# Attention with conditioned queries and keys: the order of small operations at the start and at the end of the kernel

## The chip, the cores and the metric

The kernel runs on one core of a Trainium2 chip. A core has TensorE (PE in the profile; PEld is its weight load), VectorE (DVE), ScalarE (ACT), GpSimd (POOL) and SyncE (SP, which here only issues transfers). Each engine works through its own instructions in the order in which the program issues them, and waits on semaphores for the others. The metric is the device time of one execution in microseconds (us), less is better.

## The reference, cut to what matters

```python
# x: (8, 512, 512), cond: (8, 512); 16 heads of 32
Q, K, V = heads(x @ Wq.T + bq), heads(x @ Wk.T + bk), heads(x @ Wv.T + bv)
tQ, tK  = heads(cond @ Wq.T + bq), heads(cond @ Wk.T + bk)   # one token per batch
scores  = einsum("bhqd,bhkd->bhqk", Q + tQ, K + tK) / sqrt(32)
out     = x + merge(einsum("bhqk,bhkd->bhqd", softmax(scores), V))
```

All in float32. The condition adds one vector per batch and head to every query and to every key; the residual x is added at the end.

## The kernel before

The work is cut into 32 tiles: tile t is batch t // 4 and four heads (t % 4). For each tile the kernel projects queries and keys, computes scores twice (once with queries as rows for the row maxima and the sums of exponentials, once with keys as rows for the exponentials that are multiplied with V), multiplies and stores. The main loop runs over tiles 1 to 28; the opening (tile 0 and the weights) and the last three tiles (29, 30, 31) are written out by hand. A manual schedule keeps each engine's order as written, so the place of a statement in the program is its place in the queue of its engine. The eight PSUM banks are given out by a table (`TURNS`, `banks`); a matmul that writes a bank waits for those who still read it.

Opening. TensorE first runs fillers, small matmuls whose result nobody reads (`keep_warm`, L892; `WARM = (48, 8, 8)`). x of batch 0 arrives in two halves of its rows; VectorE turns each half by two transposes of 128x512 (`turn_first_x`, L903, L908). `project` multiplies with the first columns of Wq and Wk. The second group of 8 fillers stands between the projections of the two halves, the third between the last projection of tile 0's queries and the first scores (`row_max(0, 0)`). `condition` (L863) makes tQ and tK: 32 small matmuls per weight (L870), a VectorE transpose (L878), and per group of heads one addition of `bias2` on ScalarE (L880). `bias2` is made by two VectorE scalings (L928, L929) of the turned condition (L924). W of q, k and v are turned by VectorE (`turn_w`, L342) once they have landed. Sums and differences of their blocks are made by GpSimd (`combine_w`, L361 to L364), for products of blocks in Strassen's manner, seven in place of eight: `first_products` (L496) and `other_products` (L563) issue them (L469) and put them together. In `first_products` ScalarE copies product one out of its bank (L507), then come the exponentials that were passed as `dens` (`denominators`, L682), and then what was passed as `small`. `row_max` issues the scores (L635) and VectorE's maxima (L602, L644). `split_max` (L696 to L699) cuts the maxima into three bf16 parts, which TensorE transposes (L722).

End. `crossed` (L1178 and on) interleaves the two kinds of scores for neighbouring tiles; the maxima are L1213 and L644. `part_of` (L1007) adds up the products with V: the first part of a tile is copied to SBUF by ScalarE (L1022), a later one is copied by ScalarE (L1016) and added by GpSimd (L1017). `send_parts` (L1030) divides by the sums: reciprocal (L1032), VectorE's transpose (L830), GpSimd's product and addition of the residual (L831, L832); `store` issues the transfers (L850). `add_bias` (L209, GpSimd) adds bv to the residual. For tiles 30 and 31 the sums of exponentials come from TensorE products with a matrix of ones (`times_ones`, L773) over sums that VectorE or GpSimd made first (`sum_of`, L1167, L1169). Tile 30's result is `y30`: transposed, scaled (L1294), the residual added (L1326), stored by `store_30` (L1299). Tile 31 ends with L1309 to L1341: the product and the residual added (L1319), TensorE transposes of it (L1321) and of the sums (`untranspose`, L854), the reciprocal (L1329), the scaling (L1334), and four stores (L1341).

Of the kernel before, what the change touches and what calls it, by code (L numbers as in the profile page):

```python
# [17 lines left out]
def kernel(  # L18
# [38 lines left out]
    nc = tc.nc  # L57
# [17 lines left out]
    WARM = (48, 8, 8)  # L75
# [787 lines left out]
    def condition(n, gs, pt):  # L863

        i = "qk".index(n)
        r = slice(gs[0], gs[-1] + 1)
        w = len(gs) * HD
        for cc in range(NC):
            for h in range(HG):
                nc.tensor.matmul(  # L870
                    pt[h * HD : (h + 1) * HD, :w],
                    condT[:, cc, :],
                    wT[n][:, cc, :].rearrange("p (g h e) -> p g h e", h=HG, e=HD)[:, r, h, :],
                    start=(cc == 0),
                    stop=(cc == NC - 1),
                )
        t = early[:, 1 + i, :w]
        nc.vector.transpose(t, pt[:, :w])  # L878
        for k, g in enumerate(gs):
            nc.scalar.activation(  # L880
                tok[:, i, g, :],
                t[:, k * HD : k * HD + B],
                AF.Identity,
                bias=bias2[:, i, g : g + 1],
            )
        if gs[-1] == G - 1:
            nc.gpsimd.tensor_tensor(apart_tok[:, i], tok[:, i, 1::2], tok[:, i, 0::2], ALU.subtract)
# [4 lines left out]
    def keep_warm(n):  # L892
        for _ in range(n):
            nc.tensor.matmul(warm[:, :P], onesb, onesb, start=True, stop=True)
# [8 lines left out]
    def turn_first_x(half):  # L903
        if half == 0:
            xT[0] = xtp.tile([P, NC, S], F32, tag="xT", name="xT_0")
        for k in range(2):
            cs = slice(k * 2, k * 2 + 2)
            nc.vector.transpose(  # L908
                xT[0][:, cs, two[half]].rearrange("p c (f i) -> p c f i", i=BL),
                x0[:, half_of_x[half], cs, :].rearrange("p f c e -> p c f e"),  # L910
            )
# [16 lines left out]
    nc.vector.tensor_scalar(bias2[:, 0, :], condT[:, :, B], 2.0 * SCALE, None, ALU.mult)  # L928
    nc.vector.tensor_scalar(bias2[:, 1, :], condT[:, :, B + 1], 2.0, None, ALU.mult)  # L929
# [11 lines left out]
    keep_warm(WARM[2])  # L941
# [35 lines left out]
    condition("q", [2, 3], banks(2))  # L977
    first_products("q", 0, 1, lambda: denominators(0, 1), lambda: condition("k", [2, 3], banks(3)), 1)
# [28 lines left out]
    def part_of(t, pt, of, between=None):  # L1007
# [5 lines left out]
        if t in parts:  # L1013
# [161 lines left out]
    def row(i):  # L1175
        turn[0] = 8 + i
# [43 lines left out]
    load_residual(t + 1)  # L1220
    row(4)
# [16 lines left out]
    add_bias(t - 1)  # L1238
# [7 lines left out]
    load_residual(t + 1)  # L1246
    for u in (t - 1, t, t + 1):
        add_bias(u)
    part_of(t - 1, banks(2), [2, 3])
    spread_sums(apart, banks(1))  # L1250
    den = denominators_of(t - 1, banks(1))
    row(1)
# [4 lines left out]
    send_parts(t - 1, den)  # L1257
    store()
# [26 lines left out]
    sum_of(t, acc2, 2, nc.vector)  # L1285
# [8 lines left out]
    nc.vector.tensor_tensor(y30, y30, rec.broadcast_to([P, NB, BL]), ALU.mult)  # L1294

# [8 lines left out]
    times_ones(acc2, pd, True, False)  # L1304
    times_ones([es[t, 3, pr] for pr in range(NP)], pd, False, True)
    times_v(t, 3, pv)
# [10 lines left out]
    two = [slice(0, HS), slice(HS, S)]  # L1317
    for i in range(2):
# [5 lines left out]
        if i == 0:  # L1324
            untranspose(den, pi)
    nc.vector.tensor_tensor(y30, y30, x30, ALU.add)  # L1326
    store_30(nc.sync, (0, 1))
    store_30(nc.scalar, (2,))
    nc.vector.reciprocal(  # L1329
        rec, pi.rearrange("p (c h e) -> p c h e", c=NS, h=HG)[:, :, :, 0:1]  # L1330
    )
# [13 lines left out]
    store_30(nc.scalar, (3,))  # L1345

# [30 lines left out]
```

## Time and profile before

| | |
|---|---|
| time, median of 3 runs | 664.89 us (664.83 to 665.09) |
| time of the profiled execution | 664.89 us |
| its span, first to last instruction | 663.1 us |
| mean granted TensorE clock | 0.997 |
| busy: PE / DVE / ACT / POOL | 652.7 / 578.4 / 543.2 / 338.0 us |

A row of the timeline gives start and length in us from the start of the span, the engine, the line of the kernel, the operation, the tiles written and read, and the shape; in brackets stand the idle time of the engine before it and what ended that. Instructions of one line that follow one another are merged (x8). A row of the chain of waits gives start, length, engine, tile and line: the work that, followed back from the last instruction, decided when it ended. Matmuls are pipelined and overlap, so their rows can overlap too. A q behind an engine's name is its queue: a transfer issued there.

### The profile page before, as it was taken

The numbers are of one execution on the slowest core, as the hardware profiler recorded it, in microseconds if no ns is written. First come the engines' busy times: TensorE is split into PE (matmuls) and PEld (weight loads), VectorE is DVE, ScalarE is ACT, GpSimd is POOL, SyncE is SP. The second block draws the span as 40 slices with busy tenths as digits, with TensorE's granted clock in tenths as the row PEclk, the third lists the DMA queues.
The fourth block names the chain that finished last, engine by engine and source line by source line (L and its number), as shares of the span: only waits on it lengthen the run. The fifth ranks groups of instructions, "written<-read, shape, count | busy, mean of one in ns | idle before, by whom it ended". The sixth has DMA issues, their size and how long they took to land.

```text
span 663.1 us, 22865 instructions
## 1 busy us (share of the span) xinstructions
PE 652.7 (98%) x9100; PEld 307.0 (46%) x9100; DVE 578.4 (87%) x845; ACT 543.2 (82%) x1391; POOL 338.0 (51%) x447
## 2 busy tenths in 40 slices
PE   8999999999999999999999999999999999999996
PEld 7454444544445444444544445444544545445431
DVE  5898988989798898979889898998979888897787
ACT  2479797888979888898989889798997978888673
POOL 5642543647537464565635664464744656352360
PEclk9999999999999999999999999999999999999998
DMA  9718548285665838657493865839476573830212
GB/s 210 147 33 211 119 109 211 66 219 118 158 168 123 208 73 222 132 138 184 106 223 74 205 151 129 197 75 233 95 180 154 131 185 67 214 89 16 44 33 33
DMA packets 140815, 90.86 MB, mean 137 GB/s; under 512 B 117436, under 2 KB 126308, under 8 KB 140708
## 3 DMA queue, kind: packets, MB, share of 16 engines
q1 hardware_dynamic: 132196, 73.78, 48.3%
q0 software_dynamic: 5568, 14.95, 8.8%
q8 instruction: 72, 1.18, 0.8%
q10 hardware_dynamic: 2944, 0.66, 0.5%
q14 instruction: 35, 0.29, 0.1%
HBM read 20.27 MB, written 8.39 MB: 43 GB/s over the span
## 4 chain that ended last, share of the span: by engine, by line
PE 94%; DVE 3%; issue 1%; DMA 1%; ACT 1%; ACTq 0%; DVEq 0%
PE psum L469 44%; PE psum L635 19%; PE psum L763 16%; PE psum L741 8%; PE psum L738 3%; PE psum L410 2%; DVE acc L1169 1%; DMA early<-in_x_dram 1%; DVE nmax L644 1%; PE psum L1195 1%; DVE nmax L1213 0%; DVE acc L1167 0%; PE psum L800 0%; PE psum L870 0%; ACT arena L682 0%
## 5 line engine op out<-in xcount | busy, mean ns | idle before, releaser
L602 DVE TENSOR_REDUCE nmax<-psum 128x1 f32<-128x512 f32 x326 | 205.1, 681 | 42.9 <-PE psum L635 42.4
L682 ACT ACTIVATE psum<-psum,nmax 128x512 f32<-128x512 f32 x256 | 169.3, 665 | 46.6 <-DVE nmax L602 34.5
L752 ACT ACTIVATE arena<-psum 128x512 f32<-128x512 f32 x264 | 136.3, 602 | 31.2 <-PE psum L741 22.2
L682 ACT ACTIVATE arena<-psum,nmax 128x512 f32<-128x512 f32 x224 | 152.9, 709 | 4.9 <-issue 4.2
L635 PE MATMUL psum<-kT,qT 32*128 32x512 f32 x1024 | 151.5, 619 | 0.0
L655 DVE STREAM_TRANSPOSE blocks<-blocks 128x1024 f32<-128x1024 f32 x112 | 132.3, 1220 | 0.3 <-DMA blocks<-arena 0.3
L644 DVE TENSOR_REDUCE nmax<-psum 128x2 f32<-128x1024 f32 x87 | 105.5, 1213 | 1.1 <-PE psum L635 1.1
L666 POOL DMA_DIRECT2D blocks<-arena x112 | 55.9, 504 | 72.8 <-ACT arena L682 63.6
L831 POOL TENSOR_TENSOR res<-res,recs 128x512 f32<-128x512 f32 x30 | 31.4, 1047 | 118.8 <-DVE res L830 118.8
L635 PEld LDWEIGHTS psum<-kT,qT 32*128 32x128 f32 x1024 | 55.1, 182 | 62.3 <-issue 17.4
L763 PE MATMUL psum<-arena,v 128*32 128x512 f32 x576 | 69.4, 597 | 0.0
L741 PE MATMUL psum<-qT,kT 32*128 32x512 f32 x528 | 67.9, 587 | 0.0
L682 ACT ACTIVATION_READ_ACCUMULATOR psum<-psum,nmax 128x1 f32 x256 | 52.6, 205 | 0.0
L763 PE MATMUL psum<-blocks,v 128*32 128x256 f32 x896 | 52.1, 381 | 0.0
L682 ACT ACTIVATION_READ_ACCUMULATOR arena<-psum,nmax 128x1 f32 x224 | 50.8, 227 | 0.0
L832 POOL TENSOR_TENSOR xr<-res,xr 128x512 f32<-128x512 f32 x30 | 38.4, 1279 | 2.4
L209 POOL TENSOR_TENSOR xr<-xr,wT_q 128x512 f32<-128x512 f32 x30 | 38.5, 1284 | 0.3
L763 PEld LDWEIGHTS psum<-blocks,v 128*32 128x32 f32 x896 | 26.4, 110 | 25.0 <-ACT arena L752 10.6
L830 DVE STREAM_TRANSPOSE res<-psum 128x512 f32<-128x512 f32 x28 | 20.1, 717 | 19.8 <-issue 16.0
L469 PE MATMUL psum<-wT_v,xT 128*32 128x256 f32 x512 | 34.2, 382 | 0.0
L469 PE MATMUL psum<-wc_v,xc 128*32 128x256 f32 x512 | 33.5, 379 | 0.0
L544 POOL TENSOR_TENSOR v<-v 128x512 f32<-128x512 f32 x14 | 17.9, 1277 | 29.3 <-ACT v L532 29.3
(190 smaller groups left out, 986.4 us busy)
## 6 DMA issues: line engine op xcount, KB each, us to landing
blocks<-arena SPq DMA_DIRECT2D x336, 128.0 KB, 4.1
blocks<-arena POOLq DMA_DIRECT2D x112, 128.0 KB, 4.0
xr<-in_x_dram SPq DMA_DIRECT2D x60, 128.0 KB, 2.7
x<-in_x_dram SPq DMA_DIRECT2D x56, 128.0 KB, 3.5
out_dram<-xr SPq DMA_DIRECT2D x56, 128.0 KB, 2.5
w_q<-in_L_cond_Wq_dram SPq DMA_DIRECT2D x4, 256.0 KB
w_k<-in_L_cond_Wk_dram SPq DMA_DIRECT2D x4, 256.0 KB, 7.3
w_v<-in_L_cond_Wv_dram SPq DMA_DIRECT2D x4, 256.0 KB
```

Of the source, the lines that this page charges most:

```text
L209: nc.gpsimd.tensor_tensor(xr[t], xr[t], bias, ALU.add)
L469: nc.tensor.matmul(pt[r], still[:, r], moving, start=(kc == kcs[0]), stop=(kc == kcs[-1]))
L602: nc.vector.tensor_reduce(nmax[t][:, qc, j : j + 1, 0], pt, AX.X, ALU.max, negate=True)
L635: nc.tensor.matmul(pt, qkT["q", t][r, qc * P : (qc + 1) * P], qkT["k", t][r, :], start=True, stop=True,)
L644: nc.vector.tensor_reduce(nmax[t][:, qc, pr * 2 : pr * 2 + 2, 0], pt, AX.X, ALU.max, negate=True)
L655: nc.vector.transpose(e, e)
L666: queue.dma_start(to.rearrange("p c h s -> p (c h s)"), of)
L682: nc.scalar.activation(to, of, AF.Exp, bias=nmax[t][:, qc, j, :], accum_out=sums[t][:, qc, j, :],)
L741: nc.tensor.matmul(bank[j], qkT["k", t][r, kc * P : (kc + 1) * P], qkT["q", t][r, :], start=False, stop=True,)
L752: nc.scalar.activation(e[:, i, :], bank[pr * 2 + i], AF.Exp)
L763: nc.tensor.matmul(pt[j * HD : (j + 1) * HD, at], vs[b % 2][:, kc, (g * HG + j) * HD : (g * HG + j + 1) * HD], e, start=(kc == chunks[0]), ...
L832: nc.gpsimd.tensor_tensor(xr[t], y, xr[t], ALU.add)
```

## The change

In the opening: the second group of fillers has 4 matmuls instead of 8 and the third is dropped; x's second half is turned by three transposes (two of 128x256, one of 128x512); `bias2` is made by ScalarE; and for heads 2 and 3 the additions of the condition stand behind exponentials in ScalarE's queue, those for q between the second and the third exponential of row 1, those for k behind all of `first_products`.

At the end: the residual of tile 31 is named, and bv added to the residuals of tiles 28, 29 and 31, at the start of tile 29; the last two products of tile 29 are added by one VectorE operation directly from PSUM; tile 29 is sent and stored before the next scores instead of after them; one sum of exponentials of tile 31 (chunk 2) is no longer made by VectorE, TensorE multiplies the exponentials with the ones themselves; `y30` gets its residual right after its scaling and is stored by SP in one go; tile 31's sums are transposed, and their reciprocal taken, before the second half of its result.

```diff
-    WARM = (48, 8, 8)
+    WARM = (48, 4)
...
-    def condition(n, gs, pt):
+    def condition(n, gs, pt, later=False):
...
+        def add():
+            for k, g in enumerate(gs):
+                nc.scalar.activation(tok[:, i, g, :], t[:, k * HD : k * HD + B], AF.Identity, bias=bias2[:, i, g : g + 1])
+            if gs[-1] == G - 1:
+                nc.gpsimd.tensor_tensor(apart_tok[:, i], tok[:, i, 1::2], tok[:, i, 0::2], ALU.subtract)
+        if later:
+            return add
+        add()
...
-        for k in range(2):
-            cs = slice(k * 2, k * 2 + 2)
+        for cs in ((slice(0, 1), slice(1, 2)) if half else (slice(0, 2),)) + (slice(2, 4),):
...
-    nc.vector.tensor_scalar(bias2[:, 0, :], condT[:, :, B], 2.0 * SCALE, None, ALU.mult)
-    nc.vector.tensor_scalar(bias2[:, 1, :], condT[:, :, B + 1], 2.0, None, ALU.mult)
+    for i, scale in enumerate((2.0 * SCALE, 2.0)):
+        nc.scalar.activation(bias2[:, i, :], condT[:, :, B + i], AF.Copy, scale=scale)
...
-    keep_warm(WARM[2])
...
-    condition("q", [2, 3], banks(2))
-    first_products("q", 0, 1, lambda: denominators(0, 1), lambda: condition("k", [2, 3], banks(3)), 1)
+    add_q = condition("q", [2, 3], banks(2), later=True)
+    add_k = []
+    def early_dens():
+        denominators(0, 1, js=range(2))
+        add_q()
+        denominators(0, 1, js=range(2, HG))
+    first_products("q", 0, 1, early_dens, lambda: add_k.append(condition("k", [2, 3], banks(3), later=True)), 1)
+    add_k[0]()
...
-        if t in parts:
+        if directly:
+            nc.vector.tensor_tensor(parts[t], pt, parts[t], ALU.add)
+        elif t in parts:
...
     t = T - 3
     load_residual(t + 1)
+    load_residual(t + 2)
+    for u in (t - 1, t, t + 2):
+        add_bias(u)
...
-    add_bias(t - 1)
+    add_bias(t + 1)
...
-    load_residual(t + 1)
-    for u in (t - 1, t, t + 1):
-        add_bias(u)
-    part_of(t - 1, banks(2), [2, 3])
+    part_of(t - 1, banks(2), [2, 3], directly=True)
     spread_sums(apart, banks(1))
     den = denominators_of(t - 1, banks(1))
+    send_parts(t - 1, den)
+    store()
     row(1)
...
-    send_parts(t - 1, den)
-    store()
     row(2)
...
-    sum_of(t, acc2, 2, nc.vector)
...
+    nc.vector.tensor_tensor(y30, y30, x30, ALU.add)
...
     times_ones(acc2, pd, True, False)
+    times_ones([es[t, 2, pr] for pr in range(NP)], pd, False, False)
     times_ones([es[t, 3, pr] for pr in range(NP)], pd, False, True)
+    store_30(nc.sync, range(HG))
     times_v(t, 3, pv)
...
+    untranspose(den, pi)
...
-            untranspose(den, pi)
-    nc.vector.tensor_tensor(y30, y30, x30, ALU.add)
-    store_30(nc.sync, (0, 1))
-    store_30(nc.scalar, (2,))
-    nc.vector.reciprocal(
-        rec, pi.rearrange("p (c h e) -> p c h e", c=NS, h=HG)[:, :, :, 0:1]
-    )
+            nc.vector.reciprocal(
+                rec, pi.rearrange("p (c h e) -> p c h e", c=NS, h=HG)[:, :, :, 0:1]
+            )
...
-    store_30(nc.scalar, (3,))
```

25 lines of the change are left out of this document (15 added, 10 removed).

## The prediction

> **What bounds the kernel now.** I read the page first (busy shares, chain), then the chain of waits in order of time for the first 45 us and the last 75 us, then the timeline of each engine there, because the diff touches only those two stretches.
>
> ```profile
> span 663.1 us, 22865 instructions
> PE 652.7 (98%) x9100; PEld 307.0 (46%) x9100; DVE 578.4 (87%) x845; ACT 543.2 (82%) x1391; POOL 338.0 (51%) x447
> PE 94%; DVE 3%; issue 1%; DMA 1%; ACT 1%; ACTq 0%; DVEq 0%
> ```
>
> TensorE carries 94% of the chain that ended last. So what it issues earlier in the opening moves the whole middle by the same amount; nothing in the middle is edited. In the opening the chain shows where TensorE spends time on fillers and where it leaves its own work:
>
> ```profile
> 10.80 0.45 PE psum L894 x8
> 11.25 1.94 PE psum L410 x8
> ...
> 15.80 0.45 PE psum L894 x8
> 16.25 1.07 PE psum L635 x8
> ...
> 27.74 1.13 DVE nmax L644
> ...
> 29.06 0.49 ACT tok L880 x2
> 29.55 0.27 ACT qT L507
> ...
> 29.95 1.07 PE psum L469 x16
> ...
> 32.34 3.16 PE psum L469 x56
> ```
>
> Columns: start, length, engine, tile, line. The two L894 pieces are fillers on the chain. Around 29 us the chain leaves TensorE: the condition additions (L880) wait for VectorE's row maxima (L644), and the copy of the first product (L507), queued behind them on ScalarE, holds the next product at 29.95.
>
> At the end the chain passes to VectorE at 633.8 us. These rows are of the timeline (start, length, engine, line, operation; in brackets the idle time before it and what ended it):
>
> ```profile
> 633.80 1.29 DVE L1213 TENSOR_REDUCE nmax<-psum 128x1 f32<-128x512 f32 x2 [1.62 <-PE psum L635]
> 636.30 0.65 DVE L830 STREAM_TRANSPOSE res<-parts 128x512 f32<-128x512 f32 x1
> 636.93 1.29 DVE L1213 TENSOR_REDUCE nmax<-psum 128x1 f32<-128x512 f32 x2
> 639.39 1.22 DVE L696 CAST split<-nmax 128x16 bf16<-128x16 f32 x1
> 640.86 0.20 DVE L698 CAST split<-rest 128x16 bf16<-128x16 f32 x1
> 635.84 2.36 POOL L1167 TENSOR_TENSOR acc<-arena 128x1024 f32<-128x1024 f32 x1
> 638.15 1.05 POOL L831 TENSOR_TENSOR res<-res,recs 128x512 f32<-128x512 f32 x1
> 639.28 1.26 POOL L832 TENSOR_TENSOR xr<-res,xr 128x512 f32<-128x512 f32 x1
> 641.38 0.40 PE L722 MATMUL psum<-identb,split 128*128 128x128 bf16 x4 [1.22 <-DVE split L699]
> ```
>
> See the two casts of the same size: 0.20 us at L698, but 1.22 at L696, which runs from 639.39 to 640.61 while GpSimd's addition L832 runs from 639.28 to 640.54. TensorE stands idle 1.22 us for the split that follows.
>
> **The change part by part: opening.** The rows it needs beside the chain:
>
> ```profile
> 10.43 1.30 DVE L908 STREAM_TRANSPOSE xT<-early 128x512 f32<-128x512 f32 x2 [1.67 <-DMA early<-in_x_dram]
> 11.66 0.27 DVE L924 STREAM_TRANSPOSE early<-early 128x128 f32<-128x128 f32 x1
> 13.90 0.59 ACT L880 ACTIVATE tok<-early,bias 128x8 f32<-128x8 f32 x2 [9.22 <-DVE early L878]
> 14.53 0.69 ACT L425 ACTIVATE kT<-psum,tok 128x512 f32<-128x512 f32 x1
> 29.00 0.61 PE L469 MATMUL psum<-xT,wT_q 128*32 128x256 f32 x8
> L254 SPq DMA_DIRECT2D w_k<-in_L_cond_Wk_dram x4: 902/1038/1148, 9.2 to 12.3; - x4
> w_k<-in_L_cond_Wk_dram SPq DMA_DIRECT2D x4, 256.0 KB, 7.3
> 19.71 0.71 DVE L342 STREAM_TRANSPOSE wT_k<-w_k 128x512 f32<-128x512 f32 x1
> 21.45 0.75 DVE L423 TENSOR_SCALAR qT<-psum,tok 128x512 f32<-128x512 f32 x1 [0.34 <-PE psum L410]
> 22.95 1.28 POOL L361 TENSOR_TENSOR wc_q<-wT_q 128x512 f32<-128x512 f32 x1 [6.06 <-ACT psum L682]
> 39.08 0.26 POOL L696 CAST split<-nmax 128x16 bf16<-128x16 f32 x1 [0.42 <-DVE nmax L644]
> ```
>
> Smaller pieces and four fillers fewer. The projection now waits for the first L908 piece, 10.43 + 0.65 = 11.08. A 128x256 piece lies between 0.27 (128x128) and 0.65 (128x512): 0.40 on a line, so it is there at 10.83. Eight fillers are 0.45, so four end at 10.80 + 0.23 = 11.03: the projection starts 0.22 earlier. One instruction more makes the half 2 x 0.40 + 0.65 = 1.45 instead of 1.30, so the condition's transpose (L924) ends at 12.1; its reader on TensorE, after 11.03 + 1.94 = 12.97, covers that.
>
> The two bias scalings go to ScalarE, which had stood idle 9.22 us. At a third of a us each at most (half of L880's 0.59 is the nearest row) they end by 12.7, ahead of L880 at 13.9: nothing. Without that cover they would cost their 0.6.
>
> The second filler group: 0.45. Its successor, the scores at 16.25, needs kT, ready at 14.53 + 0.69 = 15.22, less the 0.22: no wait appears. TensorE is now 0.67 ahead.
>
> Condition additions behind the exponentials. From 29.00 to 32.34 TensorE does 24 matmuls of L469 and 8 of L635. By the rows at 32.34 (3.16 / 56) and 16.25 that is 24 x 0.056 + 1.07 = 2.42; it takes 3.34, so 0.92 is waiting, first for L507, then for the banks that the late exponentials free. Now the copy runs when the first product is out, before the second one's matmuls at 29.00, and two exponentials run before the additions. The additions' readers come later on VectorE. So up to 0.92; offered in all 1.59, and at least nothing.
>
> What is late next: GpSimd. Its twelve weight combinations run without a gap from 22.95 to the split at 39.08, and had 0.42 to spare there; the split's transposes stood some 0.3 more before their turn (estimate: the split's four operations end near 40.3, TensorE's work before them at 32.34 + 3.16 + 1.07 + 3.16 + 1.07 = 40.80, two rounds of the L469 and L635 rows, less the handover). The combinations begin behind VectorE's turn of wT_q, which stands behind turning w_k at 19.71. The last w_k piece is issued at 12.3 and lands 7.3 later, 19.6, whatever the engines do. So VectorE gains about 0.06 there and 0.34 by not waiting at 21.45: GpSimd starts 0.40 earlier. The opening is worth 0.40 + 0.42 + 0.3 = 1.1 us; ends 0.7 (GpSimd no earlier) and 1.59 (never late).
>
> **End.**
>
> ```profile
> 630.74 1.92 PE L763 MATMUL psum<-arena,v 128*32 128x512 f32 x16
> 650.89 2.35 DVE L1169 TENSOR_TENSOR acc<-acc,arena 128x1024 f32<-128x1024 f32 x2
> 651.37 1.07 PE L763 MATMUL psum<-arena,v 128*32 128x512 f32 x8
> 656.16 0.76 DVE L1319 TENSOR_TENSOR late<-psum,late 128x256 f32<-128x256 f32 x2
> 656.83 0.68 DVE L1326 TENSOR_TENSOR late<-late 128x512 f32<-128x512 f32 x1
> 658.49 1.48 SPq L1341 DMA_DIRECT2D out_dram<-late  x2
> 659.74 0.65 ACTq L1299 DMA_DIRECT2D out_dram<-late  x1
> ```
>
> The part added directly (ScalarE's copy and a GpSimd addition go) costs VectorE about 0.68, as L1326, inside the 1.62 idle before 633.80: from the product's end, 632.66, to 633.4. Then `send_parts` (about 0.2 for the reciprocal and L830's 0.65) to 634.2, which delays the maxima at 633.80 by 0.4. They take 2.4 (from 633.80 to just before L830 at 636.30), so VectorE is free at 636.6. The next maxima, at 636.93, I take to wait for their scores, as the row at 633.80 does: nothing gained, and the 0.4 hidden by the 0.85 that left the place in front of them. Without that cover it would cost the 0.4.
>
> GpSimd: `add_bias` of three tiles moves to the start of tile 29, some 20 us ahead of need (uncovered it would cost three times about L832's 1.26), and the addition goes. So L831, L832 and L1167 run 634.2 + 1.05 + 1.26 + 2.36 = 638.9, done 0.5 before the cast at 639.39. The cast falls to 0.20: 1.02 at L722, within TensorE's 1.22. The bounds are 0 and 1.2. `store()` moves with it on SP, in front of nothing that is due there.
>
> The Trainium skill, "SBUF — State Buffer", section "Who interferes with whom", has a cast able to take the port pair shared with GpSimd, the second to issue being blocked for the whole instruction. By it a GpSimd operation still running at 639.39 takes all of the 1.02 back; with the trace's overlap of L696 and L832 it agrees.
>
> The last sum, 2.35 on VectorE, becomes eight matmuls. TensorE's groups are 1.92 - 1.07 = 0.85 apart, so from the product at 651.37 - 1.02 = 650.35 there are five groups: 4 x 0.85 + 1.07 = 4.47, ended 654.82, and L1319 follows near 654.9 instead of 656.16. Of the 2.35 only 1.25 - 1.02 = 0.23 arrives: TensorE is the bound now. The addition of x to y30 (0.68) and tile 30's stores go into the freed time on VectorE and SP. The reciprocal now stands before the second half's addition and waits for the sums' transposes, in the place that L1326 had; I take L1334 1.2 earlier (from 1.0 to 1.3). Last to be issued was the store at 659.74, behind two others on ScalarE's queue; now it is SP's second L1341, 658.49 + 0.74 - 1.2 - 0.1 (two stores no longer in front of it) = 657.9. So the end gives 1.85, the stores landing alike; ends 0.8 and 2.1.
>
> **Sum.** 664.89 is the profiled execution's own time and the median (span 663.1 and 1.79 around it). 664.89 - 1.1 - 1.85 = 661.94, so 661.9.
>
> **The rivals.** (B) GpSimd's chain still meets the cast: it needs only 0.5 us of delay. For it, the chain starts behind VectorE's transpose; against it, its operations have no other wait. The end gives 1.85 - 1.02 = 0.83: 664.89 - 1.1 - 0.83 = 663.0. (C) The opening is eaten by weights that land at fixed times: turning w_k at 19.71 starts within 0.1 of the landing worked out. GpSimd then starts no earlier and the opening gives 0.7, or nothing where a bank comes free late as well: 664.89 - 1.85 less 0.7 or 0, so 662.3 to 663.0. Against it, the banks' readers move earlier with the copy. B together with an opening that gives nothing: 664.89 - 0.83 = 664.1, within 0.2% (1.33 us, what a measurement can tell from no change). (D) Slower: the clock. If fewer fillers let TensorE fall to half clock in the stretch where they go, 10.80 to 16.25, its 5.45 us of work would take as long again: 664.89 - 2.95 + 5.45 = 667.4; it decides from 3 us of work at half clock. Against it, a row of the view by stretches (length, five engines' busy time with counts, then the granted clock):
>
> ```profile
> 5.50:6.80 1.30, 0.00 (x0) 0.00 (x0) 0.72 (x2) 0.00 (x0) 0.00 (x0) 1.00 0.51 152
> ```
>
> The clock is 1.00 in a stretch where TensorE does nothing for 1.3 us, and the change opens no gap as long. The Trainium skill, "TensorE: Matmul & The Clock Gate", section "What's actually happening", halves the clock after an idle window of about 3.4 us; no gap here reaches that, so by it too the fillers dropped cost nothing.
>
> **How the numbers follow.** Forecast 0.56, B 0.13, C 0.12, B with C 0.10, D and whatever like it I do not see 0.09. Faster 0.81, same 0.10, slower 0.09. Range: the best ends give 664.89 - 1.59 - 2.1 = 661.2, and 0.4 lower for what is priced low; the top is B with C, 664.1: 660.8 to 664.1. The forecast's own range is 661.2 to 662.9.
>
> **What would show it.** Right: first scores near 15.6; product seven without a gap after 29 us less 0.7; the split cast at 0.2 us with GpSimd idle; no VectorE sum after 650; the last issue near 656.8 in the new clock of the span. Wrong: a TensorE gap before the first L722 over 0.6; a cast over 1 us; L1319 less than 0.9 earlier against L722; a granted clock below 1.00 before 30 us.

## The result and the profile after

The changed kernel takes 661.48 us (median of 5 executions, 660.83 to 662.42) where the kernel before takes 664.83 in the same comparison: a ratio of 0.9948, 95% interval 0.9937 to 0.9959. The forecast was 661.9 with a range of 660.8 to 664.1. The profiled execution took 661.48 too, so the 3.41 us to the 664.89 of the profile before can be followed row by row.

The first line of the page of the kernel after, and its shares of the chain that ended last:

```profile
span 659.7 us, 22856 instructions
PE 92%; POOL 2%; DMA 2%; SPq 1%; DVE 1%; issue 1%; ACT 0%; ACTq 0%; POOLq 0%; DVEq 0%
```

TensorE still carries the chain; GpSimd, absent from it before, and the transfers, 1% of it before, have 2% each. They come in in the opening. Its rows in the timeline of the kernel after:

```profile
10.67 1.37 DVE L913 STREAM_TRANSPOSE xT<-early 128x256 f32<-128x256 f32 x3 [1.67 <-DMA early<-in_x_dram]
12.27 0.31 ACT L934 ACTIVATE bias<-early 128x4 f32<-128x4 f32 x2 [7.58 <-DVE early L929]
15.77 1.14 PE L635 MATMUL psum<-kT,qT 32*128 32x512 f32 x8
20.20 0.71 DVE L342 STREAM_TRANSPOSE wT_k<-w_k 128x512 f32<-128x512 f32 x1 [0.85 <-DMA w_k<-in_L_cond_Wk_dram]
22.16 0.69 DVE L342 STREAM_TRANSPOSE wT_q<-w_q 128x512 f32<-128x512 f32 x1
22.98 1.28 POOL L361 TENSOR_TENSOR wc_q<-wT_q 128x512 f32<-128x512 f32 x1 [5.79 <-ACT psum L682]
27.64 0.37 ACT L507 COPY qT<-psum 128x256 f32<-128x256 f32 x1 [1.80 <-PE psum L469]
28.70 0.61 PE L469 MATMUL psum<-xT,wT_q 128*32 128x256 f32 x8
29.13 1.05 PE L469 MATMUL psum<-xc,wc_q 128*32 128x256 f32 x16
39.96 0.40 PE L722 MATMUL psum<-identb,split 128*128 128x128 bf16 x4 [0.25 <-POOL split L699]
```

The copy of product one (L507) now runs at 27.64, when that product is out, and product seven (29.13) follows product two (28.70) without the wait that stood there. But GpSimd starts at 22.98, no earlier than before, because the first turn of Wk (20.20) waited 0.85 us for its transfer; and the transposes of the first split (L722) wait 0.25 us for GpSimd. They come at 39.96 instead of 40.74: the opening gave 0.78.

The end in the timeline of the kernel after:

```profile
629.06 1.92 PE L763 MATMUL psum<-arena,v 128*32 128x512 f32 x16
633.83 1.26 POOL L832 TENSOR_TENSOR xr<-res,xr 128x512 f32<-128x512 f32 x1
635.06 2.36 POOL L1188 TENSOR_TENSOR acc<-arena 128x1024 f32<-128x1024 f32 x1
637.71 0.20 DVE L696 CAST split<-nmax 128x16 bf16<-128x16 f32 x1
638.68 0.40 PE L722 MATMUL psum<-identb,split 128*128 128x128 bf16 x4 [0.20 <-DVE split L699]
652.46 0.69 DVE L1332 TENSOR_TENSOR late<-psum,xT 128x512 f32<-128x512 f32 x1 [1.25 <-PE psum L773]
653.19 0.58 ACT L1334 COPY late<-psum 128x512 f32<-128x512 f32 x1 [2.29 <-DVE late L1332]
653.26 0.42 DVE L1343 TENSOR_TENSOR late<-psum,late 128x256 f32<-128x256 f32 x1
654.59 0.26 DVE L1349 RECIPROCAL rec<-psum 128x16 f32<-128x16 f32 x1 [0.91 <-PE psum L854]
655.48 1.60 SPq L1361 DMA_DIRECT2D out_dram<-late  x2
```

GpSimd is through at 635.06 + 2.36 = 637.42, before the cast at 637.71, which now takes 0.20. From the product of 16 matmuls (L763, 629.06, before 630.74) to the end of the span it takes 30.64 us instead of 32.36: the end gave 1.72.

0.78 and 1.72 are 2.50, not 3.41. The remaining 0.90 came from the middle, where nothing is edited. The lead of the kernel after, read at the same group of TensorE's L738 in both traces (at L763 in the last column):

| start before, us | 44.23 | 201.77 | 397.62 | 515.21 | 593.41 | 630.74 |
|---|---|---|---|---|---|---|
| start after, us | 43.45 | 200.67 | 396.12 | 513.40 | 591.74 | 629.06 |
| lead | 0.78 | 1.10 | 1.50 | 1.81 | 1.67 | 1.68 |

It grows in three jumps, at 180, 365 and 493 us, and 0.14 is lost again between 515 and 593. Timeline of the kernel before at these places:

```profile
179.64 1.08 ACT L752 ACTIVATE arena<-psum 128x512 f32<-128x512 f32 x2 [0.68 <-ACT arena L682]
364.51 0.72 DVE L830 STREAM_TRANSPOSE res<-psum 128x512 f32<-128x512 f32 x1 [1.47 <-issue]
493.07 1.09 ACT L752 ACTIVATE arena<-psum 128x512 f32<-128x512 f32 x2 [0.68 <-ACT arena L682]
569.40 0.41 DVE L556 TENSOR_TENSOR kT<-psum,kT 128x256 f32<-128x256 f32 x1
```

and of the kernel after:

```profile
178.54 2.06 ACT L752 ACTIVATE arena<-psum 128x512 f32<-128x512 f32 x4 [0.40 <-ACT arena L682]
363.00 0.72 DVE L830 STREAM_TRANSPOSE res<-psum 128x512 f32<-128x512 f32 x1 [1.12 <-issue]
491.27 2.06 ACT L752 ACTIVATE arena<-psum 128x512 f32<-128x512 f32 x4 [0.40 <-ACT arena L682]
567.84 0.42 DVE L556 TENSOR_TENSOR kT<-psum,kT 128x256 f32<-128x256 f32 x1 [0.18 <-ACT arena L682]
```

A row of ScalarE is a group of four in both kernels; x2 stands where the stretch shown ends within the group. The idle time in brackets is 0.28 us longer in two ScalarE rows of the kernel before and 0.35 longer in one of VectorE: three late starts. The kernel after has one of its own, on VectorE at 567.84, which is where the 0.14 goes. What the late starts hang on is what most of the later runs ask.

### The profile page after: what moved, and what is told of

Read it like the earlier page. It is cut to its first block, busy times and chain, and to the rows that moved or that the text cites. A ratio compares the mean times of both kernels' runs of the same rounds, so it can differ in the third digit from the quotient of the medians.

```text
span 659.7 us, 22856 instructions
## 1 busy us (share of the span) xinstructions
PE 652.0 (99%) x9096; PEld 306.3 (46%) x9096; DVE 574.8 (87%) x843; ACT 542.4 (82%) x1392; POOL 337.0 (51%) x446
## 4 chain that ended last, share of the span: by engine, by line
PE 92%; POOL 2%; DMA 2%; SPq 1%; DVE 1%; issue 1%; ACT 0%; ACTq 0%; POOLq 0%; DVEq 0%
PE psum L469 43%; PE psum L635 19%; PE psum L763 17%; PE psum L741 8%; PE psum L738 3%; DMA w_k<-in_L_cond_Wk_dram 1%; SPq L254 1%; PE psum L1216 1%; DMA early<-in_x_dram 1%; PE psum L773 1%; PE psum L800 0%; ACT psum L682 0%; POOL wc_q L364 0%; POOL wc_q L361 0%; POOL wc_k L362 0%
## 5 line engine op out<-in xcount | busy, mean ns | idle before, releaser
L763 PE MATMUL psum<-arena,v 128*32 128x512 f32 x576 | 68.5, 597 | 0.0
L763 PE MATMUL psum<-blocks,v 128*32 128x256 f32 x896 | 52.1, 381 | 0.0
L832 POOL TENSOR_TENSOR xr<-res,xr 128x512 f32<-128x512 f32 x30 | 38.4, 1281 | 2.4
L763 PEld LDWEIGHTS psum<-blocks,v 128*32 128x32 f32 x896 | 26.3, 110 | 25.0 <-ACT arena L752 10.6
L830 DVE STREAM_TRANSPOSE res<-psum 128x512 f32<-128x512 f32 x28 | 20.1, 717 | 18.9 <-issue 15.6
```

Source lines behind the costliest of these rows:

```text
L763: nc.tensor.matmul(pt[j * HD : (j + 1) * HD, at], vs[b % 2][:, kc, (g * HG + j) * HD : (g * HG + j + 1) * HD], e, start=(kc == chunks[0]), ...
L832: nc.gpsimd.tensor_tensor(xr[t], y, xr[t], ALU.add)
```

## The experiments

### Opening and end apart

The kernel before with the opening's edits alone (all hunks of the diff down to `add_k[0]()`):

```diff
-    WARM = (48, 8, 8)
+    WARM = (48, 4)
...
+    add_k[0]()
```

> Only the opening's edits; the end is that of the kernel before. Theory (the opening is held by GpSimd's weight combinations and gives about 0.8 us at the first L722; what the middle gave besides, 0.9 us, were scattered stalls of the one profiled run of before): first L722 near 39.9 to 40.0 against 40.73, split cast at the end still 1.2 us, time 664.0 (663.1 to 664.2, the lower end where the middle's stalls are absent here too). Rival (the opening also takes the middle's 0.9 us away, in every run): 663.1 with no TensorE stall beyond the regular ones between 45 and 610 us. Rival (all of the offered 1.36 us arrives): first L722 at 39.4.

Measured: 664.08 us, ratio 0.9984 (0.9975 to 0.9993). In its profile the cast at the end is still 1.22 us beside GpSimd's L832. L722 of the opening stands at 40.71, hardly earlier than before, because in this execution the first scores came at 16.94 and not near 15.6. The expectation for that place was missed. The view by stretches shows why (length, busy time of TensorE, its weight loads, VectorE, ScalarE and GpSimd with counts, then the granted clock):

```profile
7.10:10.52 3.42, 3.42 (x9) 2.70 (x10) 1.44 (x3) 0.00 (x0) 0.00 (x0) 0.50 1.01 225
```

TensorE had half its clock there: the first eight products (L410) took 3.68 us instead of the 1.99 of the kernel before. That was over when the edited fillers came (12.22), so it isn't the edits' doing. Yet 0.9 us were gained later: its lead at L738 is 0.03 at 44 us and 0.94 at 593, and the three late starts of the kernel before are gone. So the theory of this expectation, that the middle's gain was chance in one profile of the kernel before, is at odds with its trace.

The end's edits alone:

```diff
-    part_of(t - 1, banks(2), [2, 3])
+    part_of(t - 1, banks(2), [2, 3], directly=True)
...
-    sum_of(t, acc2, 2, nc.vector)
```

> Only the end's edits; the opening is that of the kernel before. Theory: the cast L696 takes 0.2 us, L722 of the end stands 1.0 us nearer to tile 29's product (L763), the last store is issued 1.6 to 1.9 earlier, time 663.1 (662.9 to 663.3). Rival (the end's gain hangs on the state that the opening leaves): 664 or more. If the middle's 0.9 us came from neither half but from the run, the time scatters by as much between rounds.

Measured: 663.42 us, ratio 0.9972 (0.9963 to 0.9981). The cast is 0.20 us, L722 comes 9.63 us after L763 (before 10.64, after 9.62), and the three late starts are all there, in a second execution of that opening: the lead is the same, -0.38, through the whole middle. The two ratios multiplied give 0.9956, inside the interval of the full change. So the parts add up within the intervals, and by the traces the middle's 0.9 us belongs to the opening's edits, though it arrives long after them.

### Which part of the opening

Only the additions moved behind the exponentials (with the fillers, x's pieces and `bias2` as before):

```diff
-    condition("q", [2, 3], banks(2))
-    first_products("q", 0, 1, lambda: denominators(0, 1), lambda: condition("k", [2, 3], banks(3)), 1)
+    add_q = condition("q", [2, 3], banks(2), later=True)
...
+    add_k[0]()
```

> The kernel before, with only the condition additions of heads 2 and 3 behind ScalarE's exponentials. Theory (the order on ScalarE alone frees TensorE near 29 us, GpSimd's spare time caps it; the middle's three stalls hang on how many instructions ScalarE and VectorE were given before, which this does not change): product seven without the 0.5 us gap after product two, L361 where it was against Wk's landing, first L722 about 0.7 us earlier, and the middle keeps its three stalls (TensorE late by 0.28, 0.35 and 0.3 us near 180, 365 and 493 us). Time 0.7 us under before, 664.2 where before is 664.9. Rival (the fillers are the opening's gain): L722 as before, time unchanged.

The other three edits of the opening alone:

```diff
-    WARM = (48, 8, 8)
+    WARM = (48, 4)
...
+        for cs in ((slice(0, 1), slice(1, 2)) if half else (slice(0, 2),)) + (slice(2, 4),):
...
+        nc.scalar.activation(bias2[:, i, :], condT[:, :, B + i], AF.Copy, scale=scale)
...
-    keep_warm(WARM[2])
```

> The kernel before, with only the fillers dropped, x's second half turned in smaller pieces, and the two bias scalings on ScalarE; the condition additions stay ahead of the exponentials. Theory: first scores 0.4 us earlier, but VectorE then waits for Wk to land, ScalarE's additions still wait for VectorE's maxima, and the gap near 29 us stays; first L722 at most 0.3 us earlier. ScalarE has two instructions more and VectorE one less than before, and with the count theory the three stalls of the middle are gone, 0.9 us: time 0.9 to 1.2 us under before, 663.7 to 664.0 where before is 664.9. Rival (the stalls went with the shift in time that the additions brought): the stalls stay, time 664.6 to 664.9.

Measured: 664.15 us, ratio 0.9988 (0.9978 to 0.9998), and 664.42 us, ratio 0.9991 (0.9981 to 1.0001). Timeline around product seven, first with the additions moved:

```profile
29.57 0.61 PE L469 MATMUL psum<-xT,wT_q 128*32 128x256 f32 x8
30.00 1.05 PE L469 MATMUL psum<-xc,wc_q 128*32 128x256 f32 x16
40.51 0.40 PE L722 MATMUL psum<-identb,split 128*128 128x128 bf16 x4
```

and with the other three edits:

```profile
29.44 1.07 PE L469 MATMUL psum<-xc,wc_q 128*32 128x256 f32 x16 [0.33 <-ACT qT L507]
40.23 0.40 PE L722 MATMUL psum<-identb,split 128*128 128x128 bf16 x4
```

The gap before product seven goes with the additions and stays without them. From the first scores to L722 it takes 24.56 us before (16.18 to 40.74) and 24.56 with the three other edits (15.67 to 40.23), but 23.77 with the additions moved (16.74 to 40.51): ScalarE's order is worth 0.79. From the start of x's second half on VectorE to the first scores it takes 5.75 before (10.43 to 16.18) and 5.10 with the three edits (10.57 to 15.67): they are worth 0.65 where x's landing decides. Other profiles have up to 6.3 without them and, in the run with half the clock, 6.7 with them. Where TensorE's own queue decides, the stretch from its first product with Wk to the first scores takes 7.11 and 7.22 us in two profiles without the edits and 6.55 in six with them, 0.56 to 0.67 less.

The late starts near 180, 365 and 493 us are there with the additions moved (lead 0.23 throughout) and gone with the three others (lead 0.52 at 44 us, 1.39 at 593). The time of the three others, 664.42, missed the 663.7 to 664.0 that the count theory asked for, and its interval reaches no change; the rows carry the reading, not the time. The additions moved change no engine's number of instructions. The three others give ScalarE two more (the scalings) and take one from VectorE (two scalings less, one piece more). That fits the theory that the late starts hang on how many instructions an engine has behind it.

### Counting instructions

The kernel before with two additional one-column copies on ScalarE early in the opening, whose results nothing uses:

```diff
+    for _ in range(2):
+        nc.scalar.activation(table, table, AF.Copy, scale=1.0)
```

> The kernel before, with two more ScalarE copies of one column in the idle time after its first scaling; they compute nothing that is used. No other edit. Count theory (ScalarE's late starts near 180 and 493 us come every so many instructions of its stream, where the next block of instructions is fetched): both late starts, 0.68 us idle in front of L752 instead of 0.40, are gone there or moved to places with slack; VectorE's at 365 us stays; the opening is as before; time 0.5 us under before, 664.4 where before is 664.9. Rival (they hang on the time of the opening's end or on transfers): all three stay, time as before or 0.1 more.

Measured: 664.30 us, ratio 0.9988 (0.9979 to 0.9998), with more work than before. Its timeline at the three places (lines shifted by two):

```profile
179.40 1.08 ACT L754 ACTIVATE arena<-psum 128x512 f32<-128x512 f32 x2 [0.40 <-ACT arena L684]
364.22 0.72 DVE L832 STREAM_TRANSPOSE res<-psum 128x512 f32<-128x512 f32 x1 [1.47 <-issue]
492.47 1.58 ACT L754 ACTIVATE arena<-psum 128x512 f32<-128x512 f32 x3 [0.40 <-ACT arena L684]
```

ScalarE's two are gone from these places, VectorE's stays. Its lead at L738 is -0.07 at 44 us, 0.24 at 202 and 0.61 at 515: 0.31 and 0.37 for the two. The opening is untouched here, so a shorter opening isn't the cause.

The same for VectorE, in both directions: the kernel before with one more memset, whose result is as before, and the kernel after with one more, which gives VectorE the old number again.

```diff
     nc.vector.memset(which, 0.0)
+    nc.vector.memset(which, 0.0)
```

> The kernel before with one more memset of a small tile among VectorE's first instructions; its result is the same. Theory of the count (the late starts in the middle hang on how many instructions an engine has behind it): VectorE's turn of a result tile near 365 us, late by 1.47 us in the kernel before and by 1.12 elsewhere, starts on time, or the late start sits at the instruction ahead of it; ScalarE's late starts near 180 and 493 us (0.68 us) stay, as its count is unchanged. Time 664.5 to 664.9. Rival (the late starts hang on when the transfers of that moment collide, and moved because the opening became shorter): all three stay, 664.9.

> The kernel after with one more memset of a small tile among VectorE's first instructions, which makes VectorE's count ahead of the middle that of the kernel before again; ScalarE keeps its two additional ones. Theory of the count: the late start of VectorE's turn near 364 us comes back (1.47 us of idle time instead of 1.12) and ScalarE's two stay away; the time is 0.3 us over the kernel after, about 661.8. Rival (the shorter opening shifted the middle against its transfers): no late start comes back, 661.5.

Before with one more, at 365 us:

```profile
364.69 0.72 DVE L831 STREAM_TRANSPOSE res<-psum 128x512 f32<-128x512 f32 x1 [1.12 <-issue]
```

After with one more, at 179, 364 and 493 us:

```profile
179.41 1.09 ACT L753 ACTIVATE arena<-psum 128x512 f32<-128x512 f32 x2 [0.40 <-ACT arena L683]
364.44 0.72 DVE L831 STREAM_TRANSPOSE res<-psum 128x512 f32<-128x512 f32 x1 [1.47 <-issue]
492.73 1.09 ACT L753 ACTIVATE arena<-psum 128x512 f32<-128x512 f32 x2 [0.40 <-ACT arena L683]
```

The late start on VectorE goes with one instruction more and comes back, to the hundredth, when the old number is restored; ScalarE's follow ScalarE's number. In all these runs the two do so independently of each other. The times show less. The first was expected at 664.5 to 664.9 and took 665.45, ratio 1.0005 (0.9996 to 1.0014): in its profile the 0.33 gained near 365 is there, but the opening was 0.36 later and 0.17 more was lost at a late start that the kernel before does not have, VectorE's addition into kT at 295.72 (idle 0.20). The second took 662.46 instead of about 661.8, ratio 0.9957 (0.9943 to 0.9970), beside 0.9952 (0.9938 to 0.9966) for the kernel after. A late start of 0.3 us is shown by the rows, not by the times.

So late starts move rather than vanish, and the traces show where to. Number the records of an engine from 0, those of its sequencer (waits, issues) included. The late ones of the kernel before are ScalarE's 447 and 1343 and VectorE's 703. VectorE's in the kernel after is 1087, with one more in the kernel before it is 575, and with one more in the kernel after it is 703 again. All of these leave 63 when divided by 128. In the loop all such late starts, 22 in the 14 profiles, stand at one of these five numbers. So what stands at such a number can be late, and an edit that shifts the count puts another instruction there; most of these cost nothing that the lead shows.

The traces also tell what happens there. The page lists a queue of kind "instruction", q14, with 35 transfers; in the trace each has 8192 bytes. ScalarE, VectorE, GpSimd and SyncE together pass such a 128th record 35 times in each of the 14 profiles, and 0.67 to 1.99 us after each of the 22 late starts one of these transfers begins. So a late start comes where the engine's next instructions are about to be loaded. No run changed the loading itself, so that it costs the 0.28 to 0.35 us is inferred.

Not every small loss in the middle is of this kind. The run that sends tile 29 late, which is described below, and the kernel after with one more on VectorE lose 0.3 and 0.2 us near 280 us at no such record; what held TensorE there stays open.

### Wk's transfer and the order of the turns

The kernel after with Wq's third quarter turned before Wk's second one:

```diff
-    turn_w("k", 1)
...
+    turn_w("q", 2)
+    turn_w("k", 1)
...
-    turn_w("q", 2)
```

> The changed kernel, with VectorE's turn of the third group of Wq put ahead of its turn of Wk's second group, that is, into the time in which VectorE waits for Wk to land. Theory (GpSimd's chain starts late because VectorE stands at Wk's landing, and its end holds the first L722): the first combination L361 starts at 22.3 to 22.5 instead of 22.98, the 0.25 us wait of TensorE before the first L722 is gone, L722 at 39.6 to 39.7, time 0.3 us under the changed kernel: 661.2. Rival (TensorE is held by something else there, such as the exponentials' banks): L361 earlier, L722 still at 39.96, time 661.5.

The kernel after, unchanged, in another comparison:

> The kernel after once more, beside the run with the two orders changed. Both theories: 661.5 us, 660.8 to 662.4. What it tells is how far the end of the load of Wk moves by itself: in the runs so far the turn of its first quarter on VectorE starts between 19.5 and 20.9 us. If the opening's gain is set by that landing, the first product of tile 1 starts 17 us or so behind GpSimd's first turn of Wk whatever the time of that turn, and the 0.25 us wait for the split is there only when the landing is late; if it is set by the order of the edits, the product stands at 39.96 in both profiles.

Measured: 661.87 us, ratio 0.9948 (0.9935 to 0.9960), and 661.71 us, ratio 0.9952 (0.9938 to 0.9966): neither differs from the first result. With the turns reordered L361 came at 22.43 and L722 at 39.43 (39.6 to 39.7 expected) without a wait, as the theory had it, but the 0.3 us did not show in the time. And the second profile of the same kernel has another opening. Timeline of the kernel after, second comparison:

```profile
9.88 1.36 DVE L913 STREAM_TRANSPOSE xT<-early 128x256 f32<-128x256 f32 x3 [1.15 <-DMA early<-in_x_dram]
15.34 1.14 PE L635 MATMUL psum<-kT,qT 32*128 32x512 f32 x8
19.51 0.71 DVE L342 STREAM_TRANSPOSE wT_k<-w_k 128x512 f32<-128x512 f32 x1 [0.59 <-DMA w_k<-in_L_cond_Wk_dram]
22.29 1.27 POOL L361 TENSOR_TENSOR wc_q<-wT_q 128x512 f32<-128x512 f32 x1 [5.88 <-ACT psum L682]
39.29 0.40 PE L722 MATMUL psum<-identb,split 128*128 128x128 bf16 x4
```

With x and Wk landing earlier, L722 stands at 39.29 and not at 39.96. Put together from the timelines of eight kernels (starts in us):

| kernel | first scores | Wk's turn | GpSimd L361 | L722 | L361 less scores | L361 less Wk's turn | L722 less L361 |
|---|---|---|---|---|---|---|---|
| before | 16.18 | 19.71 | 22.95 | 40.74 | 6.77 | 3.24 | 17.79 |
| three other edits | 15.67 | 19.51 | 22.44 | 40.23 | 6.77 | 2.93 | 17.79 |
| additions moved | 16.74 | 20.36 | 23.52 | 40.51 | 6.78 | 3.16 | 16.99 |
| opening alone | 16.94 | 20.90 | 23.71 | 40.71 | 6.77 | 2.81 | 17.00 |
| turns reordered | 15.66 | 19.78 | 22.43 | 39.43 | 6.77 | 2.65 | 17.00 |
| after | 15.77 | 20.20 | 22.98 | 39.96 | 7.21 | 2.78 | 16.98 |
| after again | 15.34 | 19.51 | 22.29 | 39.29 | 6.95 | 2.78 | 17.00 |
| after, one more on VectorE | 15.91 | 21.04 | 23.83 | 40.81 | 7.92 | 2.79 | 16.98 |

GpSimd starts 6.77 us after the first scores or 2.78 after Wk's first turn, whichever is later; with ScalarE's new order L722 follows 17.0 after that. (2.65 is possible with the turns reordered, because one turn fewer stands between.) In the three rows "after" it is Wk's turn that decides, and it decides by when its transfer lands. With the turns reordered GpSimd is back at 6.77, and still the median is no better: probably because the landing and the scores lie so near each other that the 0.2 us between the two bounds is less than the executions scatter.

### The tiles' sending and the last sum

The kernel after with tile 29 sent behind the next scores again:

```diff
-    send_parts(t - 1, den)
-    store()
     row(1)
...
+    send_parts(t - 1, den)
+    store()
     row(2)
```

> The changed kernel, with tile 29's send and store put back behind the next scores. All else of the change stays, so GpSimd has as little other work as in the changed kernel, but its two operations of the send come late again. Theory (the cast waits for whatever GpSimd operation runs at its start): GpSimd does the sum L1188 first, then L831 and L832 from about 636.5 on, L832 overlaps the cast near 637.7 to 638.9, the cast takes near 1.2 us again, L722 of the end 1.0 us later, time 662.4 to 662.6. Rival (the cast was slow as VectorE's first operation of its kind there, or by the bias additions that moved): cast 0.2 us, time 661.5.

Measured: 662.43 us, ratio 0.9960 (0.9947 to 0.9974). Its timeline at the cast:

```profile
637.20 1.27 POOL L832 TENSOR_TENSOR xr<-res,xr 128x512 f32<-128x512 f32 x1
637.98 0.55 DVE L696 CAST split<-nmax 128x16 bf16<-128x16 f32 x1
639.31 0.40 PE L722 MATMUL psum<-identb,split 128*128 128x128 bf16 x4 [0.55 <-DVE split L699]
```

GpSimd meets the cast again, as it was to, but only 0.35 of the 1.02 came back at L722 (9.97 after L763, against 9.62). GpSimd's addition ends at 638.47, the cast at 638.53: the cast took what was left of the addition, and since GpSimd had less to do in front of it than before, less was left. The expected time was met by luck: the cast was to cost about 1.0 us and cost 0.35, and the profiled execution lost another 0.3 near 280 us, where nothing is edited. The Trainium skill, "SBUF — State Buffer", section "Who interferes with whom", has the later of two such operations blocked for the whole of the other. The trace agrees, and adds that the price is the remainder, 0.49 here and 1.15 in the kernel before.

The kernel after with the last sum on VectorE again:

```diff
+    sum_of(t, acc2, 2, nc.vector)
...
-    times_ones([es[t, 2, pr] for pr in range(NP)], pd, False, False)
```

> The changed kernel, with the last sum of exponentials back on VectorE and the eight matmuls with ones dropped. Theory (TensorE is the bound there, VectorE's 2.35 us were nearly hidden): TensorE waits again for VectorE before the ones, VectorE's chain to y30 runs 2.35 us later into the tail, the first result addition L1343 0.2 to 0.4 us later against L722, time 0.2 to 0.6 us over the changed kernel: 661.7 to 662.1. Rival (VectorE's sum was on the path in full): 2.35 us over, 663.8.

Measured: 662.89 us, ratio 0.9966 (0.9953 to 0.9979). Its timeline:

```profile
652.69 0.69 DVE L1316 TENSOR_TENSOR late<-late 128x512 f32<-128x512 f32 x1
653.30 0.68 DVE L1332 TENSOR_TENSOR late<-psum,xT 128x512 f32<-128x512 f32 x1
656.24 1.60 SPq L1361 DMA_DIRECT2D out_dram<-late  x2
```

The product with the residual (L1332) follows `y30`'s addition (L1316) directly and comes 14.72 after L722 (638.58), against 13.78 in the kernel after; the last stores come 0.86 later. More than expected, in the rows and in the time (661.7 to 662.1): `y30`'s addition, 0.69, now stands in front of the tail on VectorE and hides in the sum's place only if the sum is gone.

### Two orders together

Turns reordered as above, and in the tail ScalarE's copy of the sums ahead of VectorE's product that reads the same bank, with the reciprocal behind both additions:

```diff
-    part_x = late_part(10)
-    nc.vector.tensor_tensor(part_x, pd, xr[t], ALU.mult)
...
+    part_x = late_part(10)
+    nc.vector.tensor_tensor(part_x, pd, xr[t], ALU.mult)
...
-        if i == 0:
-            nc.vector.reciprocal(
-                rec, pi.rearrange("p (c h e) -> p c h e", c=NS, h=HG)[:, :, :, 0:1]
-            )
+    nc.vector.reciprocal(
+        rec, pi.rearrange("p (c h e) -> p c h e", c=NS, h=HG)[:, :, :, 0:1]
+    )
```

> The kernel after with two orders changed: the turns of Wq's third quarter stand ahead of those of Wk's second one on VectorE and GpSimd (as in the third run), and in the tail the sums of tile 31 are read from their bank by ScalarE before VectorE's product with the residual reads it, with the reciprocal behind both additions. Theory of the prediction (at the end TensorE's bank, read by two engines one after the other, sets when the reciprocal can start): ScalarE's copy of the sums, which in the kernel after waits 2.29 us and ends at 653.77, starts some 0.5 us sooner, the reciprocal moves from 0.91 us of waiting to at most 0.5, and the last issue comes 0.3 to 0.6 us sooner against the first result addition: about 0.3 to 0.6 under the kernel after, with the opening another 0 to 0.5 (the first product of tile 1 without a wait). Rival (the reciprocal isn't what the last stores wait for; the residual's product is): the last issue stays within 0.1 us of where it stands against the first result addition, and the time is that of the kernel after less 0 to 0.5 for the opening.

Measured: 661.49 us, ratio 0.9945 (0.9932 to 0.9957): no better than the kernel after. Its timeline:

```profile
652.50 0.59 ACT L1332 COPY late<-psum 128x512 f32<-128x512 f32 x1 [1.56 <-PE psum L773]
653.12 0.69 DVE L1334 TENSOR_TENSOR late<-psum,xT 128x512 f32<-128x512 f32 x1 [1.86 <-ACT late L1332]
653.91 0.76 DVE L1343 TENSOR_TENSOR late<-psum,late 128x256 f32<-128x256 f32 x2
654.58 0.25 DVE L1348 RECIPROCAL rec<-psum 128x16 f32<-128x16 f32 x1
655.39 1.62 SPq L1360 DMA_DIRECT2D out_dram<-late  x2
```

Whichever of the two reads the bank first, the other starts when it ends (653.09 and 653.12 here, 653.15 and 653.19 in the kernel after). The reciprocal loses its wait for TensorE, but stands at 654.58, where it stood at 654.59, now behind VectorE's own product and additions. The mark named for the theory, the last stores against the first result addition (L1343), moved by more than asked: 1.48 us after it instead of 2.22. But that addition itself comes 0.6 later (653.91 instead of 653.26), so the mark was badly chosen. Against L722 the last stores gain 0.13 (16.67 after it, against 16.80), and the time gains nothing: swapping the readers only moved the wait. No run of the study beats the kernel after by more than the intervals.

## Why the prediction was right, and where it was not

The forecast was 1.1 for the opening, 1.85 for the end and nothing for the middle, 2.95; measured were 0.78, 1.72 and 0.90, 3.41. The total is within 0.5 us by luck: opening and end gave 0.45 less than forecast, and the middle gave 0.90 for which the sum had no term.

**The step that failed.** "Nothing in the middle is edited", so the middle would move "by the same amount". It did not: 0.90 us were gained there. Three late starts of 0.28, 0.28 and 0.35 us left the places where TensorE waits for them, because the opening's edits give ScalarE two instructions more and VectorE one less, and one that costs 0.14 came at 568 us: in TensorE's lead 0.32, 0.40, 0.31 and -0.14. The three runs that change only the counts show that the late starts hang on them. The prediction had reckoned those instructions by their durations alone. No rival held this case.

**Opening, offered.** The smaller pieces and the fillers were put at 0.22 + 0.45 = 0.67; from x's landing to the first scores the three edits measure 0.65. ScalarE's order was put at up to 0.92; it measures 0.79. The copies of `bias2` (0.31 for two, at 12.27) are hidden as said.

**Opening, what arrives.** The cap was right in kind: GpSimd's start, behind the turn of wT_q on VectorE, and Wk's transfer before that. Its size was not. GpSimd was to start 0.40 earlier, 0.34 for VectorE's wait and 0.06 at the turn of Wk. VectorE did gain, 0.46 (3.24 to 2.78 us from that turn to GpSimd's start), but the turn came 0.49 later and not 0.06 earlier. The landing taken as 19.6 "whatever the engines do" was near 20.1 in this execution and, by the starts above, up to 21.0 in others. In the profiled pair x also landed 0.24 later, so of the 1.44 that the edits measure, 0.24 went to x and 0.42 to Wk (24.19 us from the first scores to L722, against 23.77): 0.78 is left. That is what rival (C) described, at its milder figure of 0.7. In the second profile of the same kernel, in which x came 0.55 earlier than in the kernel before, 1.45 arrived at L722. So the forecast of 1.1 lies between two executions of one kernel.

**End.** The cast: 1.02 forecast at L722, 1.02 measured (9.62 us after L763 instead of 10.64), with GpSimd through 0.3 before the cast where 0.5 was forecast; rival (B) did not occur. The run that sends tile 29 late shows its mechanism, at 0.35 instead of the 1.02 that the prediction had put on any GpSimd operation still running. Of the last sum 0.23 was to arrive: from L722 to the first result addition it takes 14.58 instead of 14.78, 0.20. TensorE became the bound there, as L1332's wait of 1.25 for L773 shows. Measured from L763 the first scaling (L1354) came 1.20 earlier, as forecast. The last issue was to begin at 657.9 instead of 659.74, 1.84 earlier; against L763 it begins 1.82 earlier (the second of the two at 655.48 begins at 656.24). The miss comes behind that: this issue takes 0.84 us where the last one before took 0.65, so the stores did not land alike, and the end of the span comes 1.72 earlier where 1.85 was forecast.

**The clock.** Rival (D) did not occur. The stretch of the fillers in the kernel after, in the view by stretches:

```profile
10.80:16.25 5.45, 5.45 (x90) 3.96 (x91) 2.73 (x8) 2.52 (x7) 4.05 (x4) 1.00 1.24 235
```

TensorE is busy through all of it and the granted clock is 1.00. The rule of the Trainium skill that the prediction cites, "TensorE: Matmul & The Clock Gate", section "What's actually happening", halves the clock after an idle window of about 3.4 us; the kernel after has none here, and nothing was lost. But the prediction read such a window as a gap without work, and no gap of that length is needed: in the run of the opening alone TensorE was idle for only 1.83 us in one piece, busy for 1.58 of the 3.41 us from 3.69 to 7.10, and then had half the clock for 3.41 us. In the kernel before with one more on VectorE it was busy for 1.63 of the 3.41 us from 4.00 on and kept the full clock.

**The list of signs.** First scores at 15.77 instead of 15.6, product seven without a gap, the cast at 0.20, no sum of VectorE after 650: right. The last issue begins at 656.24 instead of 656.8, as it must with 1.68 gained by L763 instead of 1.1. One sign against it occurred as it was written: L1319 less than 0.9 earlier against L722. It is 0.20 earlier. The sign contradicted the prediction's own sum, by which 0.23 arrives against L722 and 1.25 against L763; there it measures 1.22. No sign was named for the middle.

## What to carry to other kernels

Compare two traces at the same instruction in several places, not only where the edit is: a lead that grows in steps through unedited code has a cause of its own, and here a quarter of the gain was that. An edit that adds or removes a few small instructions early can move a late start to another instruction hundreds of us later, and gain or lose some tenths of a us there; before crediting it with a gain of that size, add instructions that compute nothing and see whether the gain comes without it. Where a bound rests on the landing of a transfer, give it the range over several executions, since one profile shows one landing.

## What was not expected of the hardware

Single instructions of ScalarE and VectorE in a regular loop start 0.26 to 0.35 us later than the same instruction elsewhere. Which one depends on the number of that engine's records ahead of it: all 22 in the 14 profiles are records 447 and 1343 of ScalarE and 575, 703 and 1087 of VectorE, 63 behind a multiple of 128, and an 8192-byte transfer of kind "instruction" follows within 2 us. Two more on ScalarE, or one more or one less on VectorE, and another instruction has that number; the old number, and the late start is back at the same place. That the loading is the cause fits all of this, but no run changed it.

TensorE had half its clock for 3.41 us in one profile, after 1.58 us of work in the 3.41 us before; 1.63 of 3.41 was enough in another. More than these two cases show about the limit was not tried.

Two engines that read one PSUM bank in the tail read it one after the other, in either order, with 0.03 to 0.04 us between them. In the traces the second reader waits for the semaphore that the first one's engine raises, so it is a wait of the program and says nothing of the bank.

The first turn of Wk started between 19.5 and 21.0 us in the profiles of kernels whose loads are the same. In their traces its last piece is issued between 11.9 and 13.0 us and lands 7.2 to 8.7 us later, so both move. What moves them stays open.
